# One signal for three PSUM banks in a graph-network kernel, and the gathers that are paced by it

## The chip, the cores and the metric

The kernel runs on one core of one Trainium2 chip. The metric is the device time of one execution in microseconds (us), as the median of several runs. The engines are named as in the profile: PE (TensorE's matmuls), PEld (its weight loads, which overlap PE), DVE (VectorE), ACT (ScalarE), POOL (GpSimd) and SP (SyncE, which issues most DMAs). The engines run in parallel, each through its own list of instructions in order, and wait for each other's signals (semaphores).

## The reference

One layer of a graph network with 6250 nodes, 206250 edges and 64 features. The edges are sorted by destination; the layer is wrapped in a normalisation ahead and a residual behind:

```python
msg = jax.nn.relu(x[src] + edge_attr)
agg = jax.ops.segment_sum(msg, dst, num_segments=x.shape[0])
h = x + agg
h = jax.nn.relu(h @ W1 + b1)
return h @ W2 + b2
...
h = jnp.maximum(_layernorm(x, axis=-1), 0.0)
x = x + _L0_gnn_ref(h, edge_index, edge_attr_64, L0_gnn_W1, L0_gnn_b1, L0_gnn_W2, L0_gnn_b2)
```

What is costly is `x[src]`: 206250 rows of 64 floats, fetched in an order that is random in the source.

## The kernel before

Edges go in 268 groups of 768 (six columns of 128 edges) and a tail. The rows `h[src]` of a group come in two ways. The first three columns are fetched from memory by indirect DMAs that POOL issues, one for each column (`gather`, L204 to L211). The other three are made on the chip: all of `h` lies in SBUF as three bf16 parts whose sum is the float (`hp`), and one-hot matmuls select rows from it. Three columns made on the chip are a *unit*. Twelve groups are made on the chip altogether; they are two units each and have no gather. There are 276 units, and `half(u)` (L730) writes the instructions of unit u for every engine, in program order.

The selection has two steps. In step one, `slots_of(k, n0)` (L527) multiplies one-hot weights `found` with `hp`, in matmuls of 32 weight columns, into one PSUM bank, `half_banks[n0 // 2 % 3]`: 20 matmuls for the first bank of a unit, 16 for each of the other two, 52 together. The last matmul is returned, so that others can wait for it. `slots_out(k, n0)` (L543) is a copy by ACT of that bank into SBUF as bf16 (`picked`). In step two, `pick(u0, cols)` (L546) multiplies `backs`, another one-hot, with `picked`, 18 matmuls into a pick bank into which `room` (L555, ACT) has already copied the edge attributes. `messages` (L627) sums the parts on DVE (L637) and applies the Relu on ACT (L639). `one_hot` (DVE) and `window_sum` (PE, L644, 12 matmuls) then sum messages by destination; `sum_into_z` (DVE, L610) adds the result into `z`.

Unit u makes the slots of a later unit (set k + 1 with k, i = divmod(u, 2)), so that the picks of unit u + 1 use slots copied one unit earlier. The order in `half(u)` is:

- POOL and SP: `enter(g + AHEAD, beats[-G + H:])` (L737) issues the loads of the group nine ahead, its three gathers among them; a source or spot load on SP.
- PE: `window_sum(u - 1)`, the slots of three banks, `pick(u + 1)`; in some units the rank matmuls of `chunk` (L790 to L800).
- ACT: `room(u + 1)`, copies of banks 1 and 2, the Relu of unit u, the copy of bank 3, then `back_near` or `back_far`.
- DVE: additions and the reduce in `messages`, `one_hot`, `sum_into_z`, `find` and `back` (the one-hot operands of later units).

What sets the order is the program order of each engine and the waits that the framework derives from data. One wait is written by hand: `beats` is a list of PE instructions, and the three gathers of a group wait for its last three entries (`behind` in `gather`, the line with reason "pace"). These entries are, in order, the last matmul of the unit's first bank (`begun`), the last matmul of its third bank, and the last matmul of the picks. They carry no data to the gather; they spread the three gathers over the unit.

Of the kernel before, what the change touches and what calls it, by code (L numbers as in the profile page):

```python
# [82 lines left out]
def kernel(  # L83
# [14 lines left out]
    nc = tc.nc  # L98
# [102 lines left out]
    beats = []  # L201
    beat = mybir.DependencyInfo(mybir.DependencyClass.Sync, mybir.DependencyReason.ANTI)
# [284 lines left out]
    backs, sources, spots, found, picked, halves, picks = {}, {}, {}, {}, {}, {}, {}  # L487

    def source_load(k):
        sources[k] = rank.tile([P, PARTS * 2 * S], I16, name="sources")  # L490
        nc.sync.dma_start(out=sources[k][:PP], in_=lines[k // SETS][k % SETS].rearrange("(o m) s -> o (m s)", o=1)
                          .to_broadcast([PP, PARTS * 2 * S]))

    def spot_load(k):
        spots[k] = rank.tile([P, 2 * H * P], BF16, name="spots")
        nc.sync.dma_start(out=spots[k], in_=spot_rows[k * 2 * H:(k + 1) * 2 * H, :]
                          .rearrange("(o t) s -> o (t s)", o=1).to_broadcast([P, 2 * H * P]))
# [29 lines left out]
    def slots_of(k, n0):  # L527
        ps = half_banks[n0 // 2 % 3][:, :2 * 3 * D].rearrange("p (u d) -> p u d", u=2)
        for u in range(2):
            i, q = divmod(n0 + u, Q)  # L530
            sets = BB + 1 if q == 0 else BB
            for b in range(sets):
                for j in range(J):
                    m = (b * PARTS + q * J) + j if b < BB else BB * PARTS + j
                    last = nc.tensor.matmul(ps[j * S:(j + 1) * S, u], found[k][:, m, i, :],  # L535
                                            hp[:, min(m, RR - 1)].rearrange("p t d -> p (t d)"),
                                            start=(b == 0), stop=(b == sets - 1))
        if n0 == 0:
            picked[k] = hot.tile([P, 2 * Q, 3 * D], BF16, name="picked")
        halves[k, n0] = ps  # L540
        return last

    def slots_out(k, n0):  # L543
        nc.scalar.copy(picked[k][:, n0:n0 + 2], halves.pop((k, n0)))  # L544

    def pick(u0, cols):  # L546
        k, i = divmod(u0, 2)
        ps = picks[u0]
        for u in cols:
            for q in range(Q):  # L550
                last = nc.tensor.matmul(ps[:, u, :3].rearrange("p t d -> p (t d)"), backs[k][:, q, i * H + u, :],  # L551
                                        picked[k][:, i * Q + q], start=False, stop=(q == Q - 1), skip_group_check=True)
        return last

    def room(u):  # L555
        g, c0 = UNITS[u]
        picks[u] = pick_banks[u % 2]
        parts = taken[g][0][:, H:].rearrange("p (t c) d -> p c t d", c=H)
        if c0:
            nc.scalar.copy(picks[u][:, :H, :3], parts)  # L560
        else:
            nc.scalar.copy(picks[u][:, :H, 0], taken[g][0][:, :H])
            nc.scalar.copy(picks[u][:, :H, 1:3], parts[:, :, 1:])

    def group_of(u):
        return UNITS[u][0] if u >= 0 else F0 + u
# [4 lines left out]
    def is_first(u):  # L571
        return u <= 0 or UNITS[u - 1][0] != UNITS[u][0]
# [37 lines left out]
    def sum_into_z(u):  # L610
        at = starts[group_of(u)]
        nc.vector.tensor_tensor(z[:, ds(at, W)], z[:, ds(at, W)], aggs.pop(u), ALU.add)  # L612

    def one_hot(u):
        g, (lo, hi) = group_of(u), span(u)
        n = hi - lo
        oh = work.tile([P, G, W], F32, name="oh", bufs=4)
        nc.vector.tensor_tensor(  # L618
            oh[:, lo:hi], slot[:, g * G + lo:g * G + hi].unsqueeze(2).to_broadcast([P, n, W]),
            slots.unsqueeze(1).to_broadcast([P, n, W]), ALU.is_equal)  # L620
        hots[u] = oh

    def enter(g, behind=()):
        if g <= NG and g not in taken:
            taken[g] = loaded[g] if g < RAW else load(g, behind[first_col(g):])

    def messages(u):  # L627
        g, (lo, hi) = group_of(u), span(u)
        ea, xg = taken[g]
        m = pool_cols(g)  # L630
        if g < RAW:
            norm_edges(xg)
        if m:
            nc.vector.tensor_tensor(ea[:, lo:m], ea[:, lo:m], xg[:, lo:m], ALU.add)  # L634
        if u >= 0:
            c0 = UNITS[u][1]
            nc.vector.tensor_reduce(ea[:, c0:c0 + H], picks.pop(u)[:, :H, :3].rearrange("p j t d -> p j d t"), AX.X, ALU.add)  # L637
        msg = work.tile([P, G, D], F32, name="msg", bufs=4)
        nc.scalar.activation(msg[:, lo:hi], ea[:, lo:hi], AF.Relu)  # L639
        msgs[u] = msg  # L640
        if is_last(u):
            taken.pop(g)

    def window_sum(u):  # L644
        (lo, hi), oh, msg = span(u), hots.pop(u), msgs.pop(u)
        pa = half_banks[0][:, 2 * 3 * D + u % AB * W:][:, :W]
        for j in range(lo, hi):
            i = (j - lo) % 2
            last = nc.tensor.matmul(pa[i * D:(i + 1) * D], msg[:, j, :], oh[:, j, :], start=(j < lo + 2), stop=(j >= hi - 2))  # L649
        if u < -1:  # L650
            beats.append(last)
        aggs[u] = pa
# [50 lines left out]
    def blocks_behind(u):  # L703
        g = group_of(u)
        for c in sorted(hid):
            res[c] = result(c, *hid.pop(c))
        for c in range(NB):
            if READY[c] == g and is_last(u):
                hid[c] = hidden(c)
# [15 lines left out]
    def is_set(k):  # L725
        return 0 <= k < KS
# [3 lines left out]
    def half(u):  # L730
        g = group_of(u)
        k, i = divmod(u, 2)
        first = ((0, 2), (6, 8))[i]
        later = ((4,), (10,))[i]
        now = is_set(k + 1)
        if is_first(u):
            enter(g + AHEAD, beats[-G + H:])  # L737
        if i == 0:
            if is_set(k + 3):
                source_load(k + 3)  # L740
        elif is_set(k + 3):
            spot_load(k + 3)
        window_sum(u - 1)
        if u + 1 < U:
            room(u + 1)
        if now:
            for n0 in first:
                begun = slots_of(k + 1, n0)
                slots_out(k + 1, n0)
                if n0 == first[0]:  # L750
                    beats.append(begun)
            for n0 in later:
                beats.append(slots_of(k + 1, n0))
        if u + 1 < U:
            blocks_behind(u - LAG - 1)
            beats.append(pick(u + 1, range(H)))
        else:
            one_hot(u)
            sum_into_z(u - LAG)
        messages(u)  # L760
        if u + 1 == U:
            sum_into_z(u - 1)
            blocks_behind(u - LAG - 1)
            return
        if u + 3 == U:
            starts_for(NG)
        if now:
            for n0 in later:
                slots_out(k + 1, n0)
        one_hot(u)  # L770
        blocks_out()
        if i == 0:
            if is_set(k + 1):
                back_near(k + 1)
                back(k + 1, 3, Q)
            sum_into_z(u - LAG)
            if is_set(k + 2):
                find(k + 2, 0)
                starts_for(group_of(u + 2))
                find(k + 2, BB)  # L780
        else:
            if is_set(k + 2):
                back_far(k + 2)
                find(k + 2, 1)
            sum_into_z(u - LAG)
            if is_set(k + 2):
                back(k + 2, 0, 1)
                starts_for(group_of(u + 2))
                back(k + 2, 1, 3)
        chunk(u + 14, rank_at)  # L790
        chunk(u + 13, rank_count)
        chunk(u + 13, rank_counted)
        chunk(u + 12, rank_of)
        chunk(u + 11, rank_marks)
        chunk(u + 11, rank_turn)
        chunk(u + 11, rank_turned)
        chunk(u + 10, rank_holds)
        chunk(u + 10, rank_fits)
        chunk(u + 9, source)
        chunk(u + 9, sourced)  # L800
        for c, to in zip(PLACED[2:], PLACED[3:]):
            if u == max(0, 2 * RG * (c // 2) - 60):
                searches.append(places(c, to))
        if g in CHECKS and is_first(u):
            searches.append(find_left(CHECKS.index(g)))
        if searches and next(searches[0], True):
            searches.pop(0)
# [111 lines left out]
    for n0 in range(0, 2 * Q, 2):  # L919
        begun = slots_of(0, n0)  # L920
# [101 lines left out]
```

## Time and profile before

| what | value |
|---|---|
| median of 3 runs | 1450.95 us (1448.59 to 1452.79) |
| the profiled execution | 1449.87 us, of which the span of the trace is 1448.1 us |
| granted TensorE clock, mean | 0.984 |
| busy share of the span | PE 79%, PEld 62%, DVE 68%, ACT 66%, POOL 56% |
| gathers in the units (L207) | 754, mean 1030 ns of POOL each |
| slot matmuls (L535) | 14352, first at 76.2 us, last at 1432.9 us of the span |

The span runs from the first to the last instruction of the profiled execution. The profile groups instructions by line; for each group it gives the count, busy time, the mean of one, and the idle time of that engine just before them with what ended it. "Issue" there stands for an idle time that no signal in the profile explains, "remote" for a signal whose giver it can't name. A timeline row gives start, length, engine, line, operation, tiles, count, and in brackets the idle time before it. Ends of matmuls are modelled. POOL's busy time is that of issuing a gather; the data move later, by DMA.

### The profile page before, as it was taken

To read this page: it belongs to the slowest core of one execution; us is meant where nothing else is said; L and a number is where in the kernel's file an instruction comes from. 1 tells how busy PE (TensorE), PEld (TensorE's weight loads), DVE (VectorE), ACT (ScalarE), POOL (GpSimd) and SP (SyncE) were. 2 spreads that over 40 slices of the span, in tenths; PEclk is the share of its full clock that TensorE was granted. 3 is DMA by queue.
4 is the path that set the end of the run, shared out by engine and by line. 5 is a ranking of instruction groups with operands and counts; after the bars stand their busy time and mean duration, and the time that the engine had idled before them with its cause. 6 is when DMAs were issued, how large, how long until landed. Compare 5 with 4: busy or idle time off the path is not lost. (4 is left out here: it accounts for less than half of the span.)

```text
span 1448.1 us, 55574 instructions
## 1 busy us (share of the span) xinstructions
PE 1144.0 (79%) x23305; PEld 901.4 (62%) x23305; DVE 977.9 (68%) x2714; ACT 955.8 (66%) x1979; POOL 810.8 (56%) x799
## 2 busy tenths in 40 slices
PE   0368888888788788888788878888878788888887
PEld 0256666666666666666666666666667666666666
DVE  8457666666677667666666667667767666766676
ACT  5457666667667667667666667666667666676676
POOL 7565556555555655655655565565565555655440
PEclk9999999999999999999999999999999999999998
DMA  5334434344344434344344434344343433444341
GB/s 176 96 108 113 139 104 122 112 135 127 102 135 117 136 111 128 104 141 119 104 129 118 139 109 127 106 130 135 99 131 115 140 107 106 135 115 138 109 113 32
DMA packets 115261, 172.42 MB, mean 119 GB/s; under 512 B 28603, under 2 KB 83772, under 8 KB 115004
## 3 DMA queue, kind: packets, MB, share of 16 engines
q1 hardware_dynamic: 89912, 143.05, 32.1%
q0 software_dynamic: 25088, 25.74, 8.3%
q8 instruction: 185, 3.03, 0.8%
q14 instruction: 72, 0.59, 0.1%
q10 hardware_dynamic: 4, 0.01, 0.0%
HBM read 164.86 MB, written 3.84 MB: 117 GB/s over the span
## 5 line engine op out<-in xcount | busy, mean ns | idle before, releaser
L207 POOL DMA_INDIRECT xg<-h_rows,src_sb x754 | 776.8, 1030 | 588.2 <-PE half L535 446.4
L535 PE MATMUL half<-hp,found 128*32 128x192 bf16 x14352 | 497.4, 248 | 225.2 <-issue 215.4
L544 ACT CAST picked<-half 128x384 bf16<-128x384 f32 x828 | 370.2, 481 | 406.6 <-remote 230.1
L535 PEld LDWEIGHTS <-found 128*32 128x32 bf16 x14352 | 317.4, 96 | 353.1 <-issue 337.6
L551 PE MATMUL pick<-picked,backs 128*128 128x192 bf16 x4968 | 468.6, 249 | 11.7 <-issue 11.5
L551 PEld LDWEIGHTS <-backs 128*128 128x128 bf16 x4968 | 402.5, 99 | 60.8 <-issue 58.2
L612 DVE TENSOR_TENSOR z<-z,half 128x32 f32 x281 | 52.9, 188 | 369.1 <-issue 177.9
L522 DVE TENSOR_SCALAR backs<-spots,ids 128x768 bf16<-128x768 int16 x690 | 258.5, 417 | 6.8 <-issue 1.2
L637 DVE TENSOR_REDUCE ea<-pick 128x192 f32<-128x576 f32 x276 | 208.2, 754 | 56.3 <-PE pick L551 38.0
L503 DVE TENSOR_SCALAR found<-sources,nodes_of 128x1536 bf16<-128x1536 int16 (+1 forms) x414 | 204.0, 521 | 0.4 <-issue 0.4
L560 ACT COPY pick<-ea 128x576 f32<-128x576 f32 x264 | 168.9, 640 | 0.0
L649 PE MATMUL half<-oh,msg 128*64 128x32 f32 x3224 | 150.5, 227 | 1.3 <-issue 1.2
L639 ACT ACTIVATE msg<-ea 128x384 f32<-128x384 f32 (+2 forms) x281 | 146.7, 522 | 6.2 <-DVE ea L637 3.1
L649 PEld LDWEIGHTS half<-oh,msg 128*64 128x64 f32 x3224 | 119.1, 138 | 45.0 <-issue 33.8
L512 ACT ACTIVATE dist<-spots,far 128x768 bf16<-128x768 int16 x138 | 130.0, 942 | 0.0
L515 ACT ACTIVATE backs<-dist,ones 128x768 bf16<-128x768 bf16 x138 | 129.6, 939 | 0.1
L618 DVE TENSOR_TENSOR oh<-slot,slots 128x192 f32<-128x192 int16 (+2 forms) x281 | 95.6, 340 | 0.0
L634 DVE TENSOR_TENSOR ea<-ea,xg 128x192 f32<-128x192 f32 x252 | 88.7, 352 | 0.0
L366 ACT CAST source<-rows 24x64 int16<-24x64 f32 x138 | 27.9, 203 | 13.5 <-PE rows L357 9.9
L339 PE MATMUL rows<-ident_b,spot_i 128*18 128x128 bf16 x46 | 10.4, 226 | 24.9 <-DVE rank_of L312 17.3
L357 PE MATMUL rows<-holds,marks 128*96 128x96 f16 x276 | 25.8, 231 | 5.1 <-ACT sp L345 5.1
L312 DVE TENSOR_REDUCE rank_of<-before 128x18 f16<-128x432 f16 x46 | 27.7, 603 | 2.2 <-issue 0.7
(110 smaller groups left out, 437.6 us busy)
## 6 DMA issues: line engine op xcount, KB each, us to landing
sources<-source_row SPq DMA_DIRECT2D x138, 384.0 KB
ea<-in_edge_attr_dram SPq DMA_DIRECT2D x268, 192.0 KB
spots<-spot_rows SPq DMA_DIRECT2D x138, 192.0 KB
xg<-h_rows,src_sb POOLq DMA_INDIRECT x754
xb<-in_x_dram SPq DMA_DIRECT2D x12, 128.0 KB
out_dram<-o SPq DMA_DIRECT2D x12, 128.0 KB
h_rows<-x SPq DMA_DIRECT2D x3, 384.0 KB
dst_sb<-in_dst_main_dram SPq DMA_DIRECT2D x1, 804.0 KB
```

What stands on the lines that cost most here:

```text
L207: it = nc.gpsimd.indirect_dma_start(out=xg[:, j, :], out_offset=None, in_=rows[:, :], in_offset=bass.IndirectOffsetOnAxis(ap=idx[:, j:j + ...
L503: nc.vector.tensor_scalar(found[k][:, b * PARTS:b * PARTS + n].rearrange("p m i s -> p (m i s)"), sources[k][:, :n * 2 * S], nodes_of[:, b ...
L512: nc.scalar.activation(dists[k], spots[k].bitcast(I16), AF.Abs, bias=far)
L515: nc.scalar.activation(backs[k][:, Q - 1].rearrange("p t s -> p (t s)"), dists.pop(k), AF.Relu, bias=ones[:, 0:1], scale=-1.0)
L522: nc.vector.tensor_scalar(backs[k][:, q].rearrange("p t s -> p (t s)"), spots[k].bitcast(I16), ids[:, q:q + 1], None, op0=ALU.is_equal)
L535: last = nc.tensor.matmul(ps[j * S:(j + 1) * S, u], found[k][:, m, i, :], hp[:, min(m, RR - 1)].rearrange("p t d -> p (t d)"), start=(b == ...
L544: nc.scalar.copy(picked[k][:, n0:n0 + 2], halves.pop((k, n0)))
L551: last = nc.tensor.matmul(ps[:, u, :3].rearrange("p t d -> p (t d)"), backs[k][:, q, i * H + u, :], picked[k][:, i * Q + q], start=False, ...
L560: nc.scalar.copy(picks[u][:, :H, :3], parts)
L637: nc.vector.tensor_reduce(ea[:, c0:c0 + H], picks.pop(u)[:, :H, :3].rearrange("p j t d -> p j d t"), AX.X, ALU.add)
L639: nc.scalar.activation(msg[:, lo:hi], ea[:, lo:hi], AF.Relu)
L649: last = nc.tensor.matmul(pa[i * D:(i + 1) * D], msg[:, j, :], oh[:, j, :], start=(j < lo + 2), stop=(j >= hi - 2))
```

## The change

The last matmul of the third bank alone is waited for, in place of that of each bank. `slots_out` gets a parameter `behind`: the copies of the first and the second bank are given a dependency on the third bank's last matmul by hand, so that PE's earlier matmuls need no signal of their own. All three copies now stand behind the unit's Relu in ACT's order, where only the third stood. The two entries of `beats` that were the first and the third bank's last matmul are now both the third bank's; the third entry, the picks, stays. The copies of the first set, ahead of the loop (L919 to L923), are untouched.

```diff
-    def slots_out(k, n0):
-        nc.scalar.copy(picked[k][:, n0:n0 + 2], halves.pop((k, n0)))
+    def slots_out(k, n0, behind=None):
+        it = nc.scalar.copy(picked[k][:, n0:n0 + 2], halves.pop((k, n0)))
+        if behind is not None:
+            tc.add_manual_dep(it.ins, behind.ins.name, beat, reason="one signal for three banks")
...
-        first = ((0, 2), (6, 8))[i]
-        later = ((4,), (10,))[i]
+        banks = ((0, 2, 4), (6, 8, 10))[i]
...
         if now:
-            for n0 in first:
-                begun = slots_of(k + 1, n0)
-                slots_out(k + 1, n0)
-                if n0 == first[0]:
-                    beats.append(begun)
-            for n0 in later:
-                beats.append(slots_of(k + 1, n0))
+            for n0 in banks:
+                last = slots_of(k + 1, n0)
+            beats.extend((last, last))
         if u + 1 < U:
             blocks_behind(u - LAG - 1)
             beats.append(pick(u + 1, range(H)))
...
         if now:
-            for n0 in later:
-                slots_out(k + 1, n0)
+            for n0 in banks:
+                slots_out(k + 1, n0, last if n0 != banks[-1] else None)
         one_hot(u)
```

## The prediction

> **What bounds the kernel now.** I began with the page: its busy shares, then its costliest groups.
>
> ```profile
> span 1448.1 us, 55574 instructions
> PE 1144.0 (79%) x23305; PEld 901.4 (62%) x23305; DVE 977.9 (68%) x2714; ACT 955.8 (66%) x1979; POOL 810.8 (56%) x799
> ...
> L207 POOL DMA_INDIRECT xg<-h_rows,src_sb x754 | 776.8, 1030 | 588.2 <-PE half L535 446.4
> L535 PE MATMUL half<-hp,found 128*32 128x192 bf16 x14352 | 497.4, 248 | 225.2 <-issue 215.4
> L544 ACT CAST picked<-half 128x384 bf16<-128x384 f32 x828 | 370.2, 481 | 406.6 <-remote 230.1
> ...
> L612 DVE TENSOR_TENSOR z<-z,half 128x32 f32 x281 | 52.9, 188 | 369.1 <-issue 177.9
> ...
> L357 PE MATMUL rows<-holds,marks 128*96 128x96 f16 x276 | 25.8, 231 | 5.1 <-ACT sp L345 5.1
> ```
>
> No engine is full. PE idles 225.2 us ahead of the slot matmuls of L535, nearly all "issue", that is, for nothing the profile names. POOL idles 588.2 us, mostly for those same matmuls. So I asked for the stretches and the timeline: a stretch with gathers against the end of the kernel, where the gathers are over.
>
> ```profile
> 76.00:700.00 624.00, 509.42 (x10509) 400.39 (x10508) 422.44 (x1178) 416.15 (x869) 358.63 (x347) 0.99 0.42 120
> ...
> 1419.00:1432.00 13.00, 13.00 (x333) 11.57 (x336) 10.94 (x31) 12.12 (x25) 0.00 (x0) 1.00 0.09 25
> ```
>
> The columns are PE, PEld, DVE, ACT, POOL, the clock and the DMA. POOL does nothing in the last row, and there PE is full. The PE timeline of that end:
>
> ```profile
> 1422.18 1.26 PE L535 MATMUL half<-hp,found 128*32 128x192 bf16 x52
> 1423.38 1.66 PE L551 MATMUL pick<-picked,backs 128*128 128x192 bf16 x18
> 1424.96 0.54 PE L649 MATMUL half<-oh,msg 128*64 128x32 f32 x12
> 1425.43 1.26 PE L535 MATMUL half<-hp,found 128*32 128x192 bf16 x52
> ```
>
> A unit takes 1425.43 - 1422.18 = 3.25 us, with its 52 slot matmuls in 1.26 us without a pause, though all three banks signal here too. A usual unit, PE, then POOL, then ACT:
>
> ```profile
> 598.64 0.54 PE L649 MATMUL half<-oh,msg 128*64 128x32 f32 x12
> 599.12 1.09 PE L535 MATMUL half<-hp,found 128*32 128x192 bf16 x27
> 600.67 0.28 PE L535 MATMUL half<-hp,found 128*32 128x192 bf16 x4 [0.46 <-issue]
> 601.40 0.66 PE L535 MATMUL half<-hp,found 128*32 128x192 bf16 x21 [0.45 <-issue]
> 602.00 1.66 PE L551 MATMUL pick<-picked,backs 128*128 128x192 bf16 x18
> ...
> 604.21 0.97 PE L535 MATMUL half<-hp,found 128*32 128x192 bf16 x25
> ```
>
> ```profile
> 596.84 1.11 POOL L207 DMA_INDIRECT xg<-h_rows,src_sb  x1 [1.11 <-PE half L535]
> 598.53 0.95 POOL L207 DMA_INDIRECT xg<-h_rows,src_sb  x1 [0.58 <-PE half L535]
> 599.78 0.95 POOL L207 DMA_INDIRECT xg<-h_rows,src_sb  x1 [0.30 <-issue]
> 601.83 0.95 POOL L207 DMA_INDIRECT xg<-h_rows,src_sb  x1 [1.10 <-PE half L535]
> 603.50 0.97 POOL L207 DMA_INDIRECT xg<-h_rows,src_sb  x1 [0.73 <-PE half L535]
> ```
>
> ```profile
> 601.59 0.86 ACT L544 CAST picked<-half 128x384 bf16<-128x384 f32 x2 [1.44 <-remote]
> 602.34 0.54 ACT L639 ACTIVATE msg<-ea 128x384 f32<-128x384 f32 x1
> 603.26 0.48 ACT L544 CAST picked<-half 128x384 bf16<-128x384 f32 x1 [0.39 <-PE half L535]
> ```
>
> Here the same 52 matmuls last from 599.12 to 602.06 = 2.94 us, and the unit 604.21 - 599.12 = 5.09 us. PE halts a few matmuls after the 20th, the first bank's last, which carries a signal. What carries its signal late: the third bank is done at 602.06, but its copy starts at 603.26, ACT idle before it, 1.43 us after the gather of 601.83 began; the next gather follows 0.24 us later. The first bank's copy waits until 601.59, with the gather of 599.78 between. So I read it thus: **while POOL issues a gather, and until about 1.43 us after its start, signals of PE don't arrive; PE itself halts when it gives one in that shadow.** After two gathers end to end (598.53, 599.78) the shadow is longer: PE runs freely again at 601.40, 1.62 us after the second's start, and the first bank's signal lets a gather go at 601.83, 2.05 us after it. What sets the pace is then a ring: gather 1 (bank 1) to gather 2 (bank 3) 598.53 - 596.84 = 1.69 us, to gather 3 (picks) 1.25 us, to the next gather 1 2.05 us; together 4.99 us. The page's 754 gathers are 251 units of three.
>
> **The change part by part.**
>
> *Two signals fewer.* In the undisturbed row 52 matmuls start within 1.26 - 0.25 (one matmul, 248 ns by the L535 row) = 1.01 us, 20 ns each, signals and all. Their own price in a unit lies between 0 and what two whole steps of matmul would be, 0.04 us: 0 to 11 us over 276 units. I take 0, since PE isn't what sets the ring. The Trainium skill, "TensorE: Matmul & The Clock Gate", section "The cost: per-tile semaphore tail", says increments are written one after another at some 26 ns each, and that one on the last matmul is sound; by it, as an estimate, two fewer in 276 units would give 14 us. It speaks for the change, and no row here shows such a tail.
>
> *Copies of banks 1 and 2 wait for bank 3, behind the Relu.* Three copies of 481 ns in a row are 1.44 us after bank 3; behind them in ACT's queue stand the far/near activation, the next room copy and, through it, the picks of the next unit. In the 5 us ring ACT has a third of its time free (66% on the page), and the next slots begin 604.21 - 602.06 = 2.15 us after bank 3: copy 1 is through by then in any case up to a signal 1.6 us late. Cost 0; if that cover goes, up to 0.48 us a unit (one copy). DVE's addition into z (L612) waits on these copies and has 369.1 / 281 = 1.3 us idle ahead of it; the columns that DVE makes and the reduce behind it move by at most the 0.47 us between bank 1's signal (601.59) and bank 3's end. Also 0.
>
> *The gathers.* This is where the time moves. Both gather 1 and 2 now wait for bank 3, so they run end to end: **1.25 instead of 1.69 us, -0.44**. Gather 1 starts 0.24 us after bank 3's signal. The picks take 1.66 us from bank 3's end, so their signal comes 1.4 us after gather 1's start, at the edge of its shadow (1.43), with gather 2 already running 0.15 us. Today the picks' signal falls clear: bank 3 ends 0.23 us *after* gather 1 has started, and the picks end at 602.00 + 1.66 = 603.66, beyond 601.83 + 1.43 = 603.26. If the signal misses the edge, it is held as bank 1's is today behind an end-to-end pair, and gather 3 starts 2.05 us after gather 2 in place of 1.25: **+0.80**. PE halts with it, free again 1.62 us after gather 2. From there the window sums (599.12 - 598.64 = 0.48) and the slots, now without a signal of their own, 1.01 to the last start: bank 3 signals 1.62 + 0.48 + 1.01 = 3.11 us after gather 2, that is 1.06 after gather 3, in its shadow, and arrives 1.43 to 1.62 after gather 3; the next gather 1 0.24 later: 1.67 to 1.86. The ring: 1.25 + 2.05 + 1.67 to 1.86 = 4.97 to 5.16. In about half of the units PE has rank matmuls beside (L357: 25.8 us in 46 units, 0.56 each; I take 0.45 over its three kinds, an estimate), which bring bank 3's signal past the shadow: 1.06 + 0.45, one matmul's 0.25 and the 0.24 to the gather make 2.0, ring 5.30. Mean of 5.07 and 5.30: 5.18.
>
> **Sum:** (5.18 - 4.99) x 251 = +48 us; units without gathers keep their 3.25. 1449.87 (the profiled execution: span 1448.1 and 1.8 around it) + 48 = 1498 us. The median of the runs, 1450.95, lies 1 us above that execution; I leave it.
>
> The Trainium skill, "SBUF — State Buffer", section "Who interferes with whom", holds that a transfer doesn't contend with a compute engine. By that alone the placing of gathers would be free and the time would stay at 1450. The two slot rows, 1.26 against 2.94 us, disagree; SBUF ports may well be innocent, for it is signals that come late.
>
> **The rivals.**
>
> *The signals were the halt (faster).* PE halts right after the first bank's signal, so without it the slots might run through in 1.26 us. If, moreover, the picks' signal gets past the edge, gather 3 follows gather 2 at once and only bank 3's signal is late: ring 1.25 + 1.25 + 2.05 = 4.55, (4.55 - 4.99) x 251 = -110: 1340 us. For it: the halt starts 5 (604.21, x25) and 7 (599.12, x27) matmuls after that signal. Against: the picks' signal must pass.
>
> *Trains of gathers hold PE (much slower).* The trace holds three gathers end to end:
>
> ```profile
> 579.83 1.02 POOL L207 DMA_INDIRECT xg<-h_rows,src_sb  x1 [0.30 <-issue]
> 581.15 0.94 POOL L207 DMA_INDIRECT xg<-h_rows,src_sb  x1 [0.30 <-issue]
> 582.40 0.95 POOL L207 DMA_INDIRECT xg<-h_rows,src_sb  x1 [0.31 <-issue]
> ```
>
> ```profile
> 577.99 0.75 PE L535 MATMUL half<-hp,found 128*32 128x192 bf16 x28
> ...
> 580.17 0.56 PE L357 MATMUL rows<-holds,marks 128*96 128x96 f16 x6
> ...
> 584.26 1.32 PE L535 MATMUL half<-hp,found 128*32 128x192 bf16 x28 [0.40 <-issue]
> 585.94 0.85 PE L535 MATMUL half<-hp,found 128*32 128x192 bf16 x16 [0.36 <-ACT pick L560]
> ```
>
> From bank 3 to bank 3 it took 586.79 - 578.74 = 8.05 us. A train needs the picks' signal to pass and PE to be held without a signal of its own. If one unit in five went so: 0.2 x 251 x (8.05 - 4.99) = +154, with the rest at 4.99 about 1600.
>
> *Nothing moves (same).* The gain of 0.44 and the loss cancel at the low end, 4.97 a unit: 1445 to 1455.
>
> **How the numbers follow.** Forecast (picks' signal caught behind the pair) 0.47, its own range 1460 to 1530, from 5.03 to 5.30 a unit; trains 0.15; signals were the halt 0.32 (a mix of its units with the forecast's fills 1340 to 1445); nothing 0.06. That is 0.62 slower, 0.32 faster, 0.06 within 0.3%, about what a measurement of this kernel can tell from no change. The range 1355 to 1620 leaves out some 0.1 of faster below and 0.08 of trains above.
>
> **What would show it.** Right: in the POOL timeline pairs 1.25 us apart after bank 3, then a third gather about 2 us later, released by the picks of L551; the "issue" idle of L535 moved to the window sums and first slots; DVE's reduce (L637) waiting for the picks far longer than now. Wrong, the fast way: 52 slot matmuls in one row of 1.26 us, with gathers running. Wrong, the other way: three gathers with 0.30 us between them and units of 6 us and more. If ACT's copies, not gathers, end the wait ahead of L535, I mis-costed the copies.

## The result, and the profile after

The changed kernel takes 1511.86 us (median of 4 runs, 1508.93 to 1514.91) against 1451.18 us of four runs of the kernel before: ratio 1.042, 95% interval 1.0388 to 1.0452. It is slower by 61 us. The profiled execution has 1509.12 us, its span is 1507.3 us.

The page of the changed kernel, the lines that answer to those shown of before (L553, L614 are the old L551, L612):

```profile
PE 1157.1 (77%) x23305; PEld 914.4 (61%) x23305; DVE 970.0 (64%) x2714; ACT 952.4 (63%) x1979; POOL 782.4 (52%) x799
...
L207 POOL DMA_INDIRECT xg<-h_rows,src_sb x754 | 748.4, 993 | 675.5 <-PE half L535 482.1
L535 PE MATMUL half<-hp,found 128*32 128x192 bf16 x14352 | 501.1, 249 | 282.1 <-issue 276.8
...
L614 DVE TENSOR_TENSOR z<-z,half 128x32 f32 x281 | 52.8, 188 | 476.1 <-ACT picked L544 417.6
```

The work is the same. PE's unexplained idle ahead of the slot matmuls has *grown*, from 215.4 to 276.8 us, though two of the banks' three signals are gone. These 61.4 us are not simply the 61 us lost: the 11.5 us of unexplained idle that stood ahead of the picks before are gone now, and PE's busy time rose by 13.1 us. POOL waits longer for the slots too. The timeline of a usual unit, PE, then POOL, then one row of DVE:

```profile
473.09 1.66 PE L553 MATMUL pick<-picked,backs 128*128 128x192 bf16 x18
...
475.31 0.67 PE L535 MATMUL half<-hp,found 128*32 128x192 bf16 x22
476.28 0.27 PE L535 MATMUL half<-hp,found 128*32 128x192 bf16 x2 [0.30 <-issue]
477.00 0.24 PE L535 MATMUL half<-hp,found 128*32 128x192 bf16 x1 [0.45 <-issue]
477.72 0.77 PE L535 MATMUL half<-hp,found 128*32 128x192 bf16 x27 [0.48 <-issue]
478.43 1.66 PE L553 MATMUL pick<-picked,backs 128*128 128x192 bf16 x18
480.02 0.54 PE L651 MATMUL half<-oh,msg 128*64 128x32 f32 x12
480.49 0.68 PE L535 MATMUL half<-hp,found 128*32 128x192 bf16 x24
```

```profile
473.43 0.94 POOL L207 DMA_INDIRECT xg<-h_rows,src_sb  x1 [1.45 <-PE half L535]
474.68 0.95 POOL L207 DMA_INDIRECT xg<-h_rows,src_sb  x1 [0.30 <-issue]
475.93 0.94 POOL L207 DMA_INDIRECT xg<-h_rows,src_sb  x1 [0.30 <-issue]
478.77 1.11 POOL L207 DMA_INDIRECT xg<-h_rows,src_sb  x1 [1.90 <-PE half L535]
480.19 1.03 POOL L207 DMA_INDIRECT xg<-h_rows,src_sb  x1 [0.30 <-issue]
```

```profile
475.71 0.74 DVE L639 TENSOR_REDUCE ea<-pick 128x192 f32<-128x576 f32 x1
```

Read the first column. The unit takes 480.49 - 475.31 = 5.18 us. The slots still halt, and in the same stretch: after 22 matmuls, where before it was 27 and 25. No matmul there carries a signal now. The whole trace agrees: of its slot rows that halt, 195 of 241 do so first after 21 to 27 matmuls, and before it was 174 of 234. The three gathers run end to end, 1.25 us apart, and the next first gather starts 478.77 - 475.93 = 2.84 us after the third: the ring is 1.25 + 1.25 + 2.84 = 5.34 us, where it was 1.69 + 1.25 + 2.05 = 4.99. The row shown is a little long. Over all gathers of the two traces the median steps are 1.71, 1.25 and 2.05 us before and 1.29, 1.25 and 2.72 us now, a ring of 5.01 and of 5.26: 0.25 us a unit, or some 63 us over 251 units, which is the loss. PE runs freely again at 477.72, 1.79 us after the third gather's start.

### The profile page after: what moved, and what is told of

The parts are those of the page before. It is cut to its first block, busy times and chain, and to the rows that moved or that the text cites. A ratio compares the mean times of both kernels' runs of the same rounds, so it can differ in the third digit from the quotient of the medians.

```text
span 1507.3 us, 54985 instructions
## 1 busy us (share of the span) xinstructions
PE 1157.1 (77%) x23305; PEld 914.4 (61%) x23305; DVE 970.0 (64%) x2714; ACT 952.4 (63%) x1979; POOL 782.4 (52%) x799
## 5 line engine op out<-in xcount | busy, mean ns | idle before, releaser
L207 POOL DMA_INDIRECT xg<-h_rows,src_sb x754 | 748.4, 993 | 675.5 <-PE half L535 482.1
L535 PE MATMUL half<-hp,found 128*32 128x192 bf16 x14352 | 501.1, 249 | 282.1 <-issue 276.8
L535 PEld LDWEIGHTS <-found 128*32 128x32 bf16 x14352 | 319.3, 96 | 410.5 <-issue 397.4
L544 ACT CAST picked<-half 128x384 bf16<-128x384 f32 x828 | 342.7, 487 | 313.3 <-PE half L535 304.6
L553 PE MATMUL pick<-picked,backs 128*128 128x192 bf16 x4968 | 481.1, 254 | 1.8 <-DVE ea L636 1.7
L553 PEld LDWEIGHTS <-backs 128*128 128x128 bf16 x4968 | 415.6, 101 | 52.1 <-issue 46.1
L614 DVE TENSOR_TENSOR z<-z,half 128x32 f32 x281 | 52.8, 188 | 476.1 <-ACT picked L544 417.6
L641 ACT ACTIVATE msg<-ea 128x384 f32<-128x384 f32 (+2 forms) x281 | 142.9, 508 | 100.7 <-DVE ea L639 62.7
L503 DVE TENSOR_SCALAR found<-sources,nodes_of 128x1536 bf16<-128x1536 int16 (+1 forms) x414 | 198.8, 508 | 0.8 <-issue 0.7
L305 ACT CAST before<-rows 128x432 f16<-128x432 f32 x46 | 23.9, 519 | 13.1 <-PE rows L298 13.0
```

Of the source, the lines that this page charges most:

```text
L207: it = nc.gpsimd.indirect_dma_start(out=xg[:, j, :], out_offset=None, in_=rows[:, :], in_offset=bass.IndirectOffsetOnAxis(ap=idx[:, j:j + ...
L503: nc.vector.tensor_scalar(found[k][:, b * PARTS:b * PARTS + n].rearrange("p m i s -> p (m i s)"), sources[k][:, :n * 2 * S], nodes_of[:, b ...
L544: it = nc.scalar.copy(picked[k][:, n0:n0 + 2], halves.pop((k, n0)))
```

## The experiments

Theory B was the prediction's own: PE halts when it gives a signal in a gather's shadow. The profile after speaks against it, so a theory A was set beside it: a gather stops PE from taking in instructions; PE works off what it already holds and halts where its program is densest; signals have no part in it. The runs were made on several chips, whose time for the kernel before differs, so each is set against the runs of before made beside it on its chip (ratios where there is an interval).

**The waits alone, and the signal alone.** The change is cut in two. From before, the gathers' waits of the change:

```diff
...
-                if n0 == first[0]:
-                    beats.append(begun)
             for n0 in later:
-                beats.append(slots_of(k + 1, n0))
+                last = slots_of(k + 1, n0)
+            beats.extend((last, last))
```

> Only the gathers' waits of the change (third bank, third bank, picks); each bank keeps its own signal and the copies of the first two banks stand where they stood. Theory A (a gather stops PE from taking in instructions, PE works off what it holds and then halts; signals have no part in it): the placing of gathers is the whole change, so 1500 to 1525 us, like the changed kernel's 1511.86. Theory B (a signal that is given in a gather's shadow halts PE): the first bank's signals are back, so slower than the changed kernel, 1530 us and more.

From the changed kernel, the gathers' old waits:

```diff
             for n0 in banks:
                 last = slots_of(k + 1, n0)
-            beats.extend((last, last))
+                if n0 != banks[1]:
+                    beats.append(last)
```

> Only the copies of the change (all three behind the third bank and the Relu); the gathers wait for first bank, third bank, picks as before, so that the first bank signals to them. Theory A: 1445 to 1460 us, the time before. Theory B: the second bank's signal is gone, the first's stays, 1440 to 1451 us. A third reading (the late copies cost something through ACT or DVE): slower than 1460 us.

Measured, with before at 1426.62 us: the waits alone 1472.09 us, ratio 1.0318 (1.0289 to 1.0347); the signal alone 1425.73 us, ratio 0.999 (0.9977 to 1.0002). The page of the run with the signal alone:

```profile
L207 POOL DMA_INDIRECT xg<-h_rows,src_sb x754 | 758.1, 1005 | 585.7 <-PE half L535 443.8
L535 PE MATMUL half<-hp,found 128*32 128x192 bf16 x14352 | 464.5, 248 | 185.5 <-issue 182.1
```

The halts of L535 stay (182.1 us) and the time is that of before. One signal a unit is gone here, the second bank's, since the first bank still signals to a gather, and the copies stand later; together they are worth nothing. That is a net figure: the window sums of this run idle 50.4 us, 26.1 of them for the addition into `z` behind a copy, where they idled 1.3 us in the profile of before. Theory B, which wanted the waits alone to be slower than the whole change, is wrong. Theory A, for which the waits were the whole change, wanted 1500 us or more, 1.034 of before, and missed by a little. Three quarters of the loss come from where the gathers stand. About 1% is missing.

**The missing 1%.** The changed kernel without the two dependencies made by hand:

```diff
-                slots_out(k + 1, n0, last if n0 != banks[-1] else None)
+                slots_out(k + 1, n0)
```

> The changed kernel without the two dependencies made by hand: each copy waits for its own bank again, but all three still stand behind the Relu, and the gathers wait for third bank, third bank, picks. The run with the waits alone was 3.2% slower than before, the whole change 4.2%. If the missing 1% comes from the copies' place behind the Relu: ratio 1.035 to 1.048. If it comes from the copies' wait for the third bank: 1.027 to 1.035.

Measured, with before at 1450.27: 1498.62 us, ratio 1.0327 (1.0303 to 1.0352), as with the waits alone. So the copies' place behind the Relu is free, and their wait for the third bank costs the last 1%; in the run with the signal alone, with the old waits of the gathers, it cost nothing that shows in the time. How it is paid is not shown. PE's unexplained idle ahead of the slots is as long here as with the whole change (274.8 and 276.8 us); the granted clock is a little higher (0.974 to 0.983 in the four runs, against 0.966 to 0.976), and whether that is a cause or a consequence is open.

**No gathers, and gathers of another kind.** Is it the gathers at all?

```diff
+            if behind:
+                it = nc.gpsimd.memset(xg[:, j, :], 0.0)
+            else:
-            it = nc.gpsimd.indirect_dma_start(
+                it = nc.gpsimd.indirect_dma_start(
...
```

> The kernel before with the paced gathers of the loop left out: POOL writes zeros into their columns instead, with the same waits. Theories A and B alike: every unit at the 3.25 us of the undisturbed end, 52 slot matmuls in one row of 1.26 us, and about 1449.9 - 251 x 1.74 = 1013 us. If PE's halts come from anything else than gathers (its own instruction supply, the waits of POOL), they stay, and the time with them, above 1300 us.

In two more runs the line in the `if` is `nc.gpsimd.dma_start(out=xg[:, j, :], in_=rows[:P, :])`, and the same with `nc.sync`:

> The kernel before, but each paced gather is a plain DMA of 128 contiguous rows, issued by POOL at the same place with the same wait (what is fetched is not x[src]). If the issuing of a DMA by POOL is what stops PE, the time stays near before, 1350 to 1440 us. If the look-up of 128 scattered rows is, it falls towards the 1044 us of the run without gathers.

> As the run with plain DMAs, but SP issues them, with the same waits and bytes. If the movement of data into SBUF is what stops PE, the time stays near before; if it is POOL's own work of issuing, 1044 to 1120 us, a little more than without gathers because SP's waits now stand ahead of its other loads.

Measured, one execution of each: 1044.53 us without gathers (before 1426.62); 1053.87 us with plain DMAs by POOL and 1042.78 us by SP (before 1450.27). The page of the run with plain DMAs by POOL:

```profile
L208 POOL DMA_DIRECT2D xg<-h_rows x748 | 432.9, 580 | 528.5 <-PE half L538 240.4
...
L538 PE MATMUL half<-hp,found 128*32 128x192 bf16 x14352 | 350.5, 247 | 4.8 <-issue 4.4
```

The halts are gone, 4.8 us of idle in place of over 200, with the same waits, the same bytes, 748 DMAs on POOL's queue and all of PE's signals. So the indirect gathers cost this kernel 1426.62 - 1044.53 = 382 us, and neither POOL's waiting, nor its issuing of a plain DMA, nor the movement of as many bytes does it. What sets an indirect gather apart is left: its list of rows, their scatter over memory, and that POOL takes 1030 ns to issue one, against 580 ns for a plain DMA.

Was each of these single executions one in which gathers would have done no harm? Their own traces say no. The 36 gathers ahead of the loop are indirect in all of them, and run until some 50 us. ACT's first copy of what PE transposes there, before and with plain DMAs by POOL:

```profile
50.50 1.17 ACT L421 COPY z<-pick 64x512 f32<-64x512 f32 x2 [4.60 <-PE rows L339]
```

```profile
51.94 1.17 ACT L424 COPY z<-pick 64x512 f32<-64x512 f32 x2 [3.87 <-remote]
```

PE's first 13 transposes are done by 42.3 us in both, and ACT idles 4.60 and 3.87 us ahead of its copy of the first eight. On a chip where gathers do no harm (the last experiment) it begins at 43.90 us, without a wait.

**PE's order made less dense.** Theory A says that halts come where the program is dense: 104 instructions in 1.0 us of slots. The kernel before, its picks dealt out between the slots (`steps` yields one pick matmul at a time):

```diff
...
+            def between():
+                waves[0] += 1
+                while len(given) < (waves[0] - 1) * H * Q // 12:
+                    given.append(next(steps))
...
-                begun = slots_of(k + 1, n0)
+                begun = slots_of(k + 1, n0, between)
```

> The kernel before with the 18 pick matmuls dealt out between the slot matmuls, one or two after every four; the gathers wait for first bank, second bank, picks. Theory A: the instructions that PE holds last longer, since slots and picks together take 2.7 us for 140 instructions in place of 1.0 us for 104 in the slots alone; a gather's shadow is mostly worked through, and the time falls to 1250 to 1400 us. Theory B: as many signals in as many shadows as before, 1440 to 1500 us.

Measured: 2647.4 us, ratio 1.8514 (1.8435 to 1.8594), far outside what either theory allowed. The stretch from 100 to 2500 us (PE, PEld, DVE, ACT, POOL, clock, DMA), then PE's timeline:

```profile
100.00:2500.00 2400.00, 2309.52 (x21656) 957.09 (x21656) 877.43 (x2416) 887.76 (x1796) 690.05 (x708) 0.50 0.24 64
```

```profile
2600.53 0.34 PE L553 MATMUL pick<-picked,backs 128*128 128x192 bf16 x1
2600.81 0.35 PE L535 MATMUL half<-hp,found 128*32 128x192 bf16 x4
2601.09 0.50 PE L553 MATMUL pick<-picked,backs 128*128 128x192 bf16 x2
```

The granted clock is 0.50 in this stretch, and four slots and a pick take 0.56 us. In the undisturbed rows of before they take some 4 x 0.02 + 1.58 / 18 = 0.17 us, which would be 0.34 at half the clock; the rest, by this estimate, is for changing between the two kinds of matmul. With its clock halved, the run says nothing on what halts cost. With only five changes in a unit the clock holds:

```diff
-            for n0 in first:
+            for j, n0 in enumerate(first + later):
                 begun = slots_of(k + 1, n0)
-                slots_out(k + 1, n0)
-                if n0 == first[0]:
+                if n0 in first:
+                    slots_out(k + 1, n0)
                     beats.append(begun)
-            for n0 in later:
-                beats.append(slots_of(k + 1, n0))
+                picks_end = pick(u + 1, range(j, j + 1))
+            beats.append(picks_end)
...
```

> The kernel before with PE's order bank 1, picks of column 1, bank 2, picks of column 2, bank 3, picks of column 3, so that the two kinds of matmul change over five times in a unit, not twelve times and more as in the run with every four dealt out, whose TensorE clock fell to half; the gathers wait for first bank, second bank, picks. Theory A (PE works off the instructions that it holds in a gather's shadow): no stretch of PE's program is as dense as 104 instructions in 1.0 us any more, so halts shrink: ratio to before 0.85 to 0.97, clock above 0.95. Theory C (changing over between 32-column and 128-column matmuls costs more than it saves): ratio above 1.0, or the clock falls again.

Measured: 1524.21 us, ratio 1.0486 (1.0448 to 1.0524), clock 0.966. Its page:

```profile
L551 PE MATMUL pick<-picked,backs 128*128 128x192 bf16 x4968 | 571.2, 253 | 262.7 <-ACT pick L560 214.2
...
L535 PE MATMUL half<-hp,found 128*32 128x192 bf16 x14352 | 465.3, 254 | 7.9 <-issue 7.7
```

The time lies where theory C put it. The halts ahead of the slots are gone, 7.9 us for 225.2, as theory A wants; in their place the picks, which now come earlier, wait 214.2 us for ACT's room copy. That copy was then moved one unit earlier (`room(u + 2)` behind the Relu of unit u), with PE's turns, and alone:

```diff
-        if u + 1 < U:
-            room(u + 1)
...
+        if u + 2 < U:
+            room(u + 2)
...
```

> The run with banks and picks by turns lost PE's halts in the slots (7.9 us idle ahead of the slot matmuls in place of 225.2) but its picks waited 214.2 us for the room copy. Here ACT makes that copy one unit earlier, behind the Relu of the unit that frees the bank. Theory A (halts come where PE's program is dense in a gather's shadow): both idle times are gone, ratio to before 0.80 to 0.92. Rival: the wait for the copy stood where halts would have stood, and they come back as issue idle ahead of slots and picks: ratio 0.93 to 1.05.

> The kernel before with the earlier room copy alone, PE's order as before. Theory A: nothing waited for that copy, and the halts in the dense slots stay: ratio 0.99 to 1.01. Rival: the earlier copy itself is worth something: below 0.98.

Measured, with before at 1449.79: with turns 1471.78 us, ratio 1.0149 (1.0129 to 1.0169); alone 1448.46 us, ratio 0.9988 (0.9978 to 0.9998). From the page of the run with turns and the early copy, and from PE's timeline at its end, where no gathers are left:

```profile
L551 PE MATMUL pick<-picked,backs 128*128 128x192 bf16 x4968 | 585.4, 251 | 41.2 <-issue 26.8
L535 PE MATMUL half<-hp,found 128*32 128x192 bf16 x14352 | 478.2, 251 | 16.9 <-issue 16.5
...
L649 PE MATMUL half<-oh,msg 128*64 128x32 f32 x3224 | 192.5, 227 | 121.7 <-ACT msg L639 55.1
```

```profile
1441.66 0.60 PE L535 MATMUL half<-hp,found 128*32 128x192 bf16 x20
...
1445.35 0.60 PE L535 MATMUL half<-hp,found 128*32 128x192 bf16 x20
```

Both idle times are nearly gone, as theory A expected, and yet no time is won: the ratio lies in the rival's range. Two payments show. An undisturbed unit now takes 1445.35 - 1441.66 = 3.69 us in place of 3.25, at a granted clock of 1.00 in both; over 276 units that would be, as an estimate, 121 us for changing over. And 121.7 us of idle stand ahead of the window sums, 55.1 of them for a Relu that comes late and 50.2 unexplained: some halts have moved there.

**A bunch in the even order.** The same kernel with the gathers' waits of the change:

> The run with turns and the early copy, with its gathers waiting for third bank, third bank, picks, as in the change. With the dense order these waits alone cost 3.2%. Theory A: there a bunch of gathers falls on the dense slots; in the even order it falls on less dense work, so it costs 0 to 2% against the run with turns and spread gathers. Rival (a bunch holds PE longer wherever it falls): 3% and more.

Measured: 1616.0 us, ratio to before 1.1146 (1.1094 to 1.1199), that is 1616.0 / 1471.78 = 1.098 against the spread gathers. From its page:

```profile
L535 PE MATMUL half<-hp,found 128*32 128x192 bf16 x14352 | 572.7, 251 | 207.3 <-issue 204.4
```

Theory A allowed 2% and missed. PE's program is as even as in the run before, and the halts ahead of the slots are back; the bunch costs more here than in the dense order.

So were the halts lost by the even order, or by gathers that stand further apart? The runs with turns changed both, since their gathers wait for the first bank, the second bank and the picks. The traces can be counted. A gather is taken as end to end with the one before when POOL idles no more than some 0.3 us between them. PE's idle is what no signal explains, from 76 us on. The few longer rows are left out.

| kernel | gathers alone | rows of two | rows of three | PE's idle, us |
|---|---|---|---|---|
| before | 271 | 211 | 8 | 229 |
| the waits alone | 29 | 25 | 219 | 250 |
| the change | 38 | 34 | 210 | 277 |
| turns | 663 | 27 | 5 | 39 |
| turns, early copy | 450 | 130 | 6 | 95 |
| turns, early copy, bunched | 10 | 6 | 238 | 250 |

Before, 201 of the 229 us begin while the second gather of a row is the last one started (222 of these), and only 15 us behind the 492 gathers that stand alone or first. With turns and the early copy it is 53 us behind 137 second gathers, 0.39 us each in place of 0.91. Behind third gathers it is 206 us for 210 in the change and 183 us for 238 in the bunched even order, 0.98 and 0.77 us each. So in either order most of PE's halts stand behind gathers end to end, and an even order makes them shorter. A gather alone over the dense slots halts PE too, but for less: the change has 34 such, with 12 us. No run keeps the gathers apart in the dense order, so what each of the two is worth in time stays open.

**Indices in order.** What of an indirect gather is it, the form or the scatter?

```diff
+    in_order = const.tile([P, 1], I32, name="in_order")
+    nc.gpsimd.iota(in_order, pattern=[[0, 1]], base=0, channel_multiplier=1)
...
-                in_offset=bass.IndirectOffsetOnAxis(ap=idx[:, j:j + 1], axis=0))
+                in_offset=bass.IndirectOffsetOnAxis(ap=in_order[:, :1] if behind else idx[:, j:j + 1], axis=0))
```

> The kernel before, its paced gathers still indirect, but with a list of indices that names rows 0 to 127 in order, the same for each (what is fetched is not x[src]). The run with plain DMAs of the same 128 rows by POOL took 1053.87 us. If the indirect form of the instruction is what stops PE (POOL reads a list and makes a descriptor for each row), the time stays within 3% of before. If the scatter of the rows over memory is, it falls to 1050 to 1150 us.

Measured, in one execution: 1053.83 us. But on this run's chip the kernel *before*, with its scattered gathers, took 1055.55 us, also in one execution. The timeline of the run with indices in order, PE, then POOL, then ACT ahead of the loop:

```profile
504.38 0.54 PE L651 MATMUL half<-oh,msg 128*64 128x32 f32 x12
504.85 1.26 PE L537 MATMUL half<-hp,found 128*32 128x192 bf16 x52
506.04 1.66 PE L553 MATMUL pick<-picked,backs 128*128 128x192 bf16 x18
```

```profile
502.89 0.95 POOL L209 DMA_INDIRECT xg<-h_rows,in_order  x1 [0.30 <-PE half L537]
504.14 1.16 POOL L209 DMA_INDIRECT xg<-h_rows,in_order  x1 [0.30 <-issue]
505.61 1.25 POOL L209 DMA_INDIRECT xg<-h_rows,in_order  x1 [0.30 <-PE half L537]
```

```profile
43.90 1.97 ACT L423 COPY z<-pick 64x512 f32<-64x512 f32 x4
```

Gathers end to end, and 52 slot matmuls in 1.26 us beneath them. The 36 gathers ahead of the loop have their scattered rows here too, and yet ACT's first copy begins at 43.90 us, where it was 50.50 and 51.94. By this row and the two times no halts and no late signals are there on this chip whatever the indices, so the run can't tell form from scatter; the question stays open, and so does what the chips differ in. The changed kernel was not run on that chip.

## Why the prediction was right, and where its steps were wrong

The prediction said 1498 us, forecast range 1460 to 1530, slower with 0.62; it came to 1511.86. The sum was right, its mechanism only in part, and that the number came out so near is luck in part: two of its steps were wrong and nearly cancel.

- *The ring of gathers bounds the kernel, not an engine:* right. Without gathers 1044.53 for 1426.62 us; and the waits of the gathers alone make 1.0318 of the 1.042.
- *Two signals fewer are worth nothing:* not contradicted, 0.999 for the run with one signal fewer. By the 26 ns an increment of the Trainium skill ("TensorE: Matmul & The Clock Gate", section "The cost: per-tile semaphore tail") one fewer in 276 units would give, as an estimate, 276 x 0.026 = 7 us or 0.5%. The interval reaches only to 0.23% below before, so no such gain is seen; but the copies moved in that run too, so it is not a clean test of the rule.
- *The copies' order is worth nothing:* right with the old waits and for the place behind the Relu (1.0327 against 1.0318). With the new waits of the gathers the dependency on the third bank costs about 1%, which the sum did not have.
- *Gathers 1 and 2 end to end, 1.69 to 1.25 us:* right, 474.68 - 473.43, and 1.29 in the median.
- *The picks' signal is caught, +0.80 between gathers 2 and 3:* wrong. The third follows at once, 475.93 - 474.68 = 1.25 us, as in the median. The picks ended 473.09 + 1.66 - 473.43 = 1.32 us after gather 1 began, a little inside the 1.43 us of the prediction's shadow, and yet their signal passed: DVE's reduce, which reads them, began at 475.71, ahead of gather 3.
- *The slots run through without a signal of their own, 1.67 to 2.0 us from gather 3 to the next gather 1:* wrong, it is 2.84 in the row shown and 2.72 in the median. This is the step that failed at its root: "PE itself halts when it gives one in that shadow". That the halt began a few matmuls after a signal was true of the rows and was not the cause; with the signal gone it begins in the same stretch. What the runs showed in its place is that PE halts behind gathers end to end, whether it signals or not: 206 of its 277 us behind third gathers. Why it does was not found.

The two errors are -0.80 and, by the median, +0.72 to +1.05 us a unit: ring 5.26, where the prediction had 4.97 to 5.30. Of the rivals, "the signals were the halt" fell with this result. "Trains of gathers hold PE" described the pattern better than the forecast did, and its sign, three gathers with 0.30 us between them, is what came; only the units are of 5.26 us and not of 6 and more. It took its 8.05 us from a row that holds four gathers end to end: one of 578.43, which the prediction does not show, stands ahead of its three.

The rule cited from the Trainium skill, "SBUF — State Buffer", section "Who interferes with whom", that a transfer doesn't contend with a compute engine, is borne out in one half: plain DMAs of the same bytes leave PE alone (1053.87 and 1042.78 us). By it alone the placing of the gathers would have been free, and it cost 3.2%; the measurement decides. Whether the halts have to do with SBUF at all, no run shows.

## What to carry to other kernels

Where a wait paces transfers and carries no data, it is a setting of its own: cut it out of a change and measure it alone; here two waits made three quarters of the loss of a change that was meant for signals. An idle time that begins just behind some instruction is not yet caused by it: take that instruction away and see whether the idle time stays. Where one edit moves two things, as the turns moved PE's order and the gathers, count in the traces which of the two the effect goes with. When idle time disappears and the time doesn't, look for what was paid for it: here 0.44 us a unit for changing the kind of matmul four times more.

## What the runs showed of the hardware

- Indirect gathers by POOL, above all two or three end to end, halted PE and delayed its signals on the chips of most runs (382 us of 1426.62), and plain DMAs by POOL did not (4.8 us of idle). On one other chip the same kernel took 1055.55 us, and the run beside it has gathers end to end above unbroken slots. What makes the difference was not found.
- In the run that changed between 32-column and 128-column matmuls after every four slots and one or two picks, the granted TensorE clock was 0.50 over 2400 us, with PE busy for 2309.52 of them; with five changes in a unit it was 0.966.
